# RWKV block on one core: the own part of the recurrence in one column-tiled piece, the deviation spread by small transfers, products on GpSimd, and an order given as turns

## The chip, the core and the metric

The kernel runs on one core of a Trainium2 chip. The core has five engines, each with its own instruction queue that is worked off in order: TensorE (PE in the profile; PEld is its weight load), VectorE (DVE), ScalarE (ACT), GpSimd (POOL) and SyncE (SP), which here issues nearly all DMA transfers. The metric is the device time of one launch in microseconds. Before the change three runs took 729.16, 731.47 and 731.89 us; their median is 731.47 us.

## The reference

One RWKV layer over a batch of NB = 8 sequences of T = 256 tokens with E = 512 channels, all in float32. H = 32 heads have S = 16 channels each. Every batch starts from a state of its own.

```
xn = ln(x) * ln1_w + ln1_b;   sx = shift(xn) - xn
xxx = tanh((xn + sx * maa_x) @ maa_w1)            # five groups of 32
x5 = xn + sx * (maa_stack + xxx @ maa_w2)         # five mixed inputs
w = exp(-exp(time_decay + tanh(x5[1] @ decay_w1) @ decay_w2))
r, k, v = x5[3] @ Wr.T, x5[0] @ Wk.T, x5[2] @ Wv.T
g = silu(x5[4] @ Wg.T)
for t in range(T):                                # per head, s is 16 x 16
    a = outer(k[t], v[t])
    out[t] = r[t] @ (u * a + s)                   # u = faaaa
    s = a + w[t] * s
att = (out - mean) * rsqrt(var + eps) * gn_w + gn_b   # per head, 16 channels
x = x + (att * g) @ Wo.T
xn2 = ln(x) * ln2_w + ln2_b;  sx2 = shift(xn2) - xn2
rr = sigmoid((xn2 + sx2 * ffn_maa_r) @ ffn_Wr.T)
kk = relu((xn2 + sx2 * ffn_maa_k) @ ffn_Wk.T) ** 2
return x + rr * (kk @ ffn_Wv.T)
```

In `out[t]` the term with `u * a` needs no state: it is (sum over the head's channels of r·u·k) times v. It is called the own part below.

## The kernel before

**Layout.** Channels lie on the 128 partitions and tokens along the free axis. The 512 channels are four blocks of 128 (blk), taken in two halves q of two blocks m, so a tile of 128 x 2 x 256 holds half of a batch's tensor. k and v have one column more, a leading one, so that they are also read shifted by a token. Within a block r, k and w are stored with the head as the fast index of the partition, v and att with another order in which each head's channels stand in four groups of 32 partitions.

**Stages.** For each batch there are three stages. `inputs_of_scan` loads x, normalizes it, builds the mixed inputs (PE L608, DVE L617, POOL L619) and projects them (PE L540). `scan` runs the recurrence. `rest` normalizes per head, multiplies by the gate, projects with Wo, and runs the feed-forward part with weights that are streamed from memory for each batch into tiles Ws (PE L540 and L555). In phase p the planner may mix the inputs of batch p, the scan of batch p-1 and the rest of batch p-2.

**The scan.** v goes to a DRAM tile vo (a transfer issued by ACT), and for each block four transfers on SP (L368, the helper's `dma_start`) read it back, spread over partitions, as vs, 512 KB each. ACT L699 writes the first column of vs, DVE L702 multiplies vs with kp (in PSUM) into kv, DVE L704 runs the recurrence over 1024 columns into st, POOL L707 multiplies it by r. When the four pieces of a block are done, PE L715 sums over channels ("gather") into one half of the PSUM tile pat, and DVE L721 adds that to att. For the own part, POOL L685 multiplies r by k, a block at a time, PE L687 sums over the head with a full 128 x 128 mask hm (scaled by faaaa) into the other half of pat, and DVE L689 multiplies by v into att. There are four vs buffers, five st (st8), three att and one pat; `ps`, the pool for all other products, has three buffers.

**The deviation.** In `rest`, ACT squares att (L729), PE L736 averages the squares per head in four column tiles of 32 outputs each, one for each block, so that the result has 128 rows for the four blocks; ACT and DVE turn it into the reciprocal deviation rs (L741, L743). PE L750 spreads rs back over the channels of each head with selection masks in `con`, and DVE L757 multiplies att by it. ACT L760 applies gn_w and gn_b, POOL L762 multiplies by the gate.

**The order.** Every piece of work is recorded with an engine and a cost in us, and `Plan.order` makes a static order for all five queues, which is then emitted. `AIMS` gives each piece an aim, as numbers written into the kernel. For each engine the planner looks at the next 14 ready pieces (`AHEAD`), takes the one with the least sum of earliest start and `PULL` times aim, and among the engines the one that can start first. `safe` keeps it from taking buffers in a way that could block.

Of the kernel before, what the change touches and what calls it, by code (L numbers as in the profile page):

```python
# [10 lines left out]
ALU = mybir.AluOpType  # L11

P = 128
NB, T, E = 8, 256, 512
H, S = 32, 16
# [15 lines left out]
C_HM, C_MEAN = 0, P  # L31
# [26 lines left out]
class Plan:  # L58
# [4 lines left out]

    LATENCY = {"PE": 0.25, "DVE": 0.12, "ACT": 0.2, "POOL": 0.15, "DMA": 2.6}
    SWITCH = {"ACT": 1.3, "PE": 0.1}
    AHEAD = 14
# [32 lines left out]
    def stage(self):  # L99
# [5 lines left out]
    AIMS = """  # L105
        -172 35 -38 12 -58 44 -27 96 7 17 28 24 132 62 53 37 25 19 18 194 65 220 8 -18 5 -33 -10 -4 -14 -2
        8 136 74 286 35 35 95 34 10 214 26,
        -186 -106 -126 -144 -123 -108 -71 -55 -105 -91 -92 -149 -126 -130 -97 -116 -129 -42 -103 -116 -154
        -126 -118 -6 -12 2 -49 -3 -7 -57 -40 -48 -50 -64 -58 -55 -58 -10 -3 -65 -58 -51 -28 -71 -61 91 12
        4 -363 5 -8 22 32 -10 22 32 45 22 73 30 22 24 30 49 33 9 11 3 -59 20 -1 11 7 19 -3 -13 -8 -9 -5 8  # L110
        16 -2 30 21 10 26 65 38 70 69 50 21 18 16 43 18 44 22 32 6 40 34 42 56,
        30 18 23 20 21 -6 -4 25 -44 -32 21 7 -6 34 23 28 34 35 -41 20 10 35 23 31 41 15 55 5 24 46 34 50
        53 51 53 53 55 59 30 -18 73 4 63 -33 -11 62 -37 42 16 69 90 85 97 57 95 118 106 128 115 101 67 101
        74 106 101 93 62 78 -75 71 97 75 91 14 19 102 43 52 88 57 107 86 75 101 89 104 125 129 117 110 120
        115 -30 40 111 -51 -2 75 151 133 131 142 147 153,
        32 41 24 26 25 3 12 27 13 57 51 42 -4 36 88 11 55 11 -63 66 84 81 58 66 99 105 66 103 98 18 124
        118 99 84 80 118 -39 34 131 -30 52 97 107 14 50 145 -40 20 57 140 146 146 156 117 158 168 161 169
        173 127 119 158 121 152 154 123 -7 24 53 15 51 128 153 99 102 151 121 136 145 119 130 155 138 170
        180 171 175 163 184 253 175 94 110 151 129 106 116 158 135 199 184 87 188 200,
        37 -9 36 36 159 135 183 163 107 51 134 38 95 161 143 171 187 185 94 180 185 193 172 176 185 198  # L120
        168 184 190 187 192 265 188 181 172 199 198 206 217 185 194 202 197 155 193 247 169 193 158 186
        232 229 241 199 207 253 240 232 244 150 174 231 181 253 241 210 241 243 177 225 227 246 223 252
        243 248 233 238 248 237 210 218 254 249 253 262 264 239 140 277 282 276 223 217 152 189 221 216
        253 230 238 252 270 283,
        174 178 166 199 155 188 210 268 184 279 224 264 257 279 276 292 298 289 152 278 282 297 276 285
        247 300 289 297 299 296 309 287 294 282 273 306 312 316 318 319 313 287 311 235 262 350 326 324 75
        283 322 325 326 306 319 345 351 345 341 292 307 333 268 294 335 307 282 290 248 324 311 308 311
        348 338 341 334 337 332 216 267 329 331 345 341 321 285 333 321 353 335 310 360 360 348 351 349
        326 273 294 373 283 318 382,
        281 278 270 328 330 288 340 354 258 298 309 287 275 356 277 342 376 375 295 273 368 375 362 369  # L130
        371 373 370 371 380 376 390 386 375 366 361 383 366 378 364 364 384 306 379 355 383 414 409 402
        338 418 411 410 422 381 410 433 439 431 437 378 406 414 384 397 419 412 417 409 321 430 409 408
        410 412 418 410 404 418 406 380 420 422 439 436 419 412 458 436 435 478 445 443 382 390 434 346
        374 418 441 451 459 441 450 465,
        359 355 361 343 374 358 405 409 363 373 376 361 357 418 408 442 435 454 371 425 440 442 448 447
        434 450 442 442 445 439 442 451 453 426 425 471 384 430 479 450 479 446 473 453 461 436 484 478
        479 463 489 474 500 458 498 514 494 502 518 474 518 502 476 442 464 497 379 454 387 479 467 483
        473 494 487 469 486 486 473 473 468 496 478 499 529 487 487 503 492 493 540 507 524 546 513 549
        550 518 503 545 559 514 533 550,
        416 412 423 422 424 375 477 509 425 478 512 449 432 518 411 525 528 514 464 492 547 531 531 538  # L140
        530 529 517 521 541 540 387 507 533 525 492 535 488 557 559 482 547 517 512 466 508 561 534 553
        441 549 547 560 574 538 576 559 582 577 599 569 570 544 556 586 548 557 548 548 411 572 577 509
        557 538 563 555 574 575 539 484 567 529 584 604 588 581 585 591 586 591 585 574 441 492 529 344
        463 535 607 597 627 634 591 601,
        -75 -13 35 -2 34 48 26 39 75 -14 39 41 44 78 -3 38 48 27 53 71 45 28 31 80 75 43 66 76 51 36 29 33
        60 100 78 72 86 57 72 61 80 86 76 25 8 104 73 43 -13 125 80 82 70 -34 -14 55 69 40 30 59 82 35 78
# [72 lines left out]
    def sequence(self, phases):  # L219
        self.ops = []  # L220
        rows = [row.split() for row in self.AIMS.split(",")]
        for p, phase in enumerate(phases):
# [3 lines left out]
            for kind, i in phase:  # L226
# [3 lines left out]
                for op, op.rank in zip(lot, map(int, aims)):  # L230
                    pass
# [664 lines left out]
```

## Time and profile before

| what | us | share of the span |
|---|---|---|
| median of three runs | 731.47 | |
| the profiled execution | 735.19 | |
| its span, first to last instruction | 733.1 | |
| PE busy | 673.4 | 92% |
| DVE busy | 595.4 | 81% |
| POOL busy | 558.0 | 76% |
| ACT busy | 345.6 | 47% |
| own part on PE, DVE, POOL (L687, L689, L685) | 20.3, 13.0, 20.5 | |
| spreading the deviation on PE, DVE (L750, L757) | 9.1, 10.5 | |

The granted clock of PE was 0.968 of full speed over the span. A busy time is what an engine's instructions cover; since matmuls overlap, the mean of one matmul is longer than the time that it adds. An idle time ("idle before") belongs to the engine in front of the instruction, and behind the arrow stands what ended it.

### The profile page before, as it was taken

The page shows a single profiled execution, that of the slowest core. Times are in us where ns is not written, and L with a number is a line of the kernel's source. Part 1 is how long each engine was busy: PE and PEld are TensorE (multiplying, and loading weights), DVE is VectorE, ACT ScalarE, POOL GpSimd, SP SyncE. Part 2 cuts the span into 40 slices and gives each one's busy share as a digit, 9 for nine tenths or more (in the row PEclk, how much of TensorE's full clock was granted, in tenths as well). Part 3 has the DMA queues.
Part 4 walks back from the last instruction along what each step waited for, and adds up shares of the span by engine and source line. Part 5 has one row for each costly group of instructions (what it writes and reads, how often), then busy time and mean ns, then how long its engine had stood idle before and what let it go on. Part 6 is the DMA issues. An engine that isn't in the chain of part 4 may idle for free. (4 is left out here: it accounts for less than half of the span.)

```text
span 733.1 us, 10498 instructions
## 1 busy us (share of the span) xinstructions
PE 673.4 (92%) x3744; PEld 446.6 (61%) x3744; DVE 595.4 (81%) x612; ACT 345.6 (47%) x705; POOL 558.0 (76%) x462
## 2 busy tenths in 40 slices
PE   4899699889989989999999999999988999799997
PEld 3676376647756567547764686648755666545453
DVE  1559999999999998889699978999888799798120
ACT  4256334335755156524773555626634236434441
POOL 4557976887996788878887997789876778779351
PEclk9899799989999998999999999999999799999999
DMA  8686456447666567763958539662973338873542
GB/s 294 230 233 170 116 136 148 99 110 203 168 159 187 176 160 185 180 212 99 218 169 245 173 100 259 161 190 86 252 211 98 87 99 212 221 218 113 173 143 86
DMA packets 53891, 124.23 MB, mean 169 GB/s; under 512 B 7440, under 2 KB 12432, under 8 KB 53840
## 3 DMA queue, kind: packets, MB, share of 16 engines
q1 hardware_dynamic: 49232, 119.38, 59.6%
q10 hardware_dynamic: 4608, 4.20, 1.9%
q8 instruction: 29, 0.48, 0.3%
q14 instruction: 22, 0.18, 0.1%
HBM read 115.16 MB, written 8.39 MB: 169 GB/s over the span
## 5 line engine op out<-in xcount | busy, mean ns | idle before, releaser
L707 POOL TENSOR_TENSOR st<-st,r 128x1024 f32<-128x1024 f32 x128 | 301.5, 2359 | 75.7 <-DVE st L704 71.4
L704 DVE TENSOR_TENSOR_SCAN st<-wrep,kv 128x1024 f32<-128x1024 f32 x128 | 292.0, 2281 | 8.4 <-PE pat L715 1.2
L702 DVE TENSOR_TENSOR kv<-vs,kp 128x1024 f32<-128x1024 f32 x128 | 156.7, 1224 | 19.6 <-ACT vs L699 16.6
L555 PE MATMUL ps<-Ws,mix 128*128 128x512 f32 x256 | 117.6, 600 | 5.4 <-DMA Ws<-in_fr 2.5
L619 POOL TENSOR_TENSOR mix<-mix,xn 128x512 f32<-128x512 f32 x80 | 86.4, 1092 | 28.5 <-DVE mix L617 26.4
L699 ACT ACTIVATE vs<-s,cm 128x4 f32<-128x4 f32 x128 | 38.1, 298 | 135.7 <-DMA vs<-vo 133.6
L617 DVE SCALAR_TENSOR_TENSOR mix<-ps,vec,sx 128x256 f32<-128x256 f32 x160 | 68.5, 474 | 20.2 <-PE ps L608 13.9
L555 PEld LDWEIGHTS ps<-Ws,mix 128*128 128x128 f32 x256 | 46.8, 190 | 59.2 <-issue 48.0
L715 PE MATMUL pat<-st,con 128*32 128x256 f32 x1024 | 68.8, 395 | 3.2 <-DVE att L689 2.3
L540 PE MATMUL ps<-mix,Wk 128*128 128x256 f32 x256 | 65.0, 405 | 2.8 <-DVE att L757 2.1
L540 PE MATMUL ps<-mix,Wg 128*128 128x256 f32 x256 | 61.4, 394 | 2.4 <-DVE mix L617 1.6
L540 PE MATMUL ps<-mix,Ws 128*128 128x256 f32 x256 | 59.1, 383 | 3.4 <-ACT g L663 1.7
L540 PE MATMUL ps<-mix,Wr 128*128 128x256 f32 x256 | 60.5, 383 | 1.3 <-ACT w L645 0.6
L540 PEld LDWEIGHTS ps<-mix,Wk 128*128 128x128 f32 x256 | 50.0, 201 | 15.4 <-issue 6.1
L540 PE MATMUL ps<-mix,Wv 128*128 128x256 f32 x256 | 59.0, 381 | 0.0
L555 PE MATMUL ps<-Ws,g 128*128 128x512 f32 x128 | 58.0, 599 | 0.9 <-DMA Ws<-in_wo 0.5
L540 PEld LDWEIGHTS ps<-mix,Wg 128*128 128x128 f32 x256 | 49.5, 197 | 12.8 <-issue 2.4
L540 PEld LDWEIGHTS ps<-mix,Ws 128*128 128x128 f32 x256 | 47.8, 190 | 13.8 <-POOL mix L527 3.8
L540 PEld LDWEIGHTS ps<-mix,Wr 128*128 128x128 f32 x256 | 47.6, 190 | 11.7 <-issue 3.9
L527 POOL TENSOR_TENSOR mix<-mix,xn 128x512 f32<-128x512 f32 x48 | 51.7, 1092 | 3.9 <-ACT mix L525 3.9
L715 PEld LDWEIGHTS pat<-st,con 128*32 128x32 f32 x1024 | 32.6, 112 | 36.3 <-issue 8.5
L540 PEld LDWEIGHTS ps<-mix,Wv 128*128 128x128 f32 x256 | 48.1, 190 | 9.2 <-issue 2.5
(79 smaller groups left out, 839.1 us busy)
## 6 DMA issues: line engine op xcount, KB each, us to landing
vs<-vo SPq DMA_DIRECT2D x128, 512.0 KB, 4.8
Ws<-in_wo SPq DMA_DIRECT2D x32, 256.0 KB, 4.6
Ws<-in_fv SPq DMA_DIRECT2D x32, 256.0 KB, 4.4
Ws<-in_fk SPq DMA_DIRECT2D x32, 256.0 KB, 4.4
Ws<-in_fr SPq DMA_DIRECT2D x32, 256.0 KB, 4.2
xt<-in_x SPq DMA_DIRECT2D x16, 256.0 KB, 4.4
x<-in_x SPq DMA_DIRECT2D x16, 256.0 KB, 4.8
vo<-v ACTq DMA_DIRECT2D x32, 128.0 KB, 4.6
```

Source lines behind the costliest of these rows:

```text
L527: gp(512, t, [t, xn[q]], lambda q=q, t=t: nc.gpsimd.tensor_tensor(t(), t(), xn[q]()[:, :, 1 : T + 1], ALU.add), 1.8)
L540: nc.tensor.matmul(ps()[:, m, :], lhsT=w[k]()[:, o : o + P], rhs=src[k // 2]()[:, k % 2, :], start=(k == 0), stop=(k == NK - 1),)
L555: nc.tensor.matmul(ps().rearrange("p m t -> p (m t)"), lhsT=src[h]()[:, k % 2, n * P : (n + 1) * P], rhs=w[k](), start=(k == 0), stop=(k = ...
L617: dve(256, [t], [p_, vec, sx[q]], lambda g=g, q=q, m=m, t=t, p_=p_: nc.vector.scalar_tensor_tensor(t()[:, m, :], p_()[:, m, :], col(f"maa_ ...
L619: gp(512, t, [t, xn[q]], lambda q=q, t=t: nc.gpsimd.tensor_tensor(t(), t(), xn[q]()[:, :, 1 : T + 1], ALU.add), 1.8)
L699: act(4, vs, [s0, cm], lambda i=i, blk=blk, vs=vs: nc.scalar.activation(vs()[:, :, 0:1], s0()[:, blk, 4 * i : 4 * i + 4].rearrange("p (n o ...
L702: dve(4 * T, [kv], [vs, kp], lambda m=m, vs=vs, kv=kv, kp=kp: nc.vector.tensor_tensor(kv(), vs(), kp()[:, m : m + 1, :].to_broadcast([P, 4 ...
L704: dve(4 * T, [st], [w, kv], lambda w=w, kv=kv, st=st: nc.vector.tensor_tensor_scan(st().rearrange("p n t -> p (n t)"), w().rearrange("p n ...
L707: gp(4 * T, st, [st, r], lambda m=m, st=st, r=r: nc.gpsimd.tensor_tensor(st(), st(), r()[:, m : m + 1, :].to_broadcast([P, 4, T]), ALU.mult))
L715: nc.tensor.matmul(pat()[32 * i : 32 * i + 32, 0, :], lhsT=con()[:, s : s + 32], rhs=done[i]()[:, j, :], start=(j == 0), stop=(j == 3),)
```

## The change

The own part is computed for a whole batch at once: two products r·k of double width on POOL, one piece on PE of four column tiles (masks of 32 columns, one tile for each block) into a `ps` tile, and a copy on ACT to a tile c, whose row block of 32 partitions holds what one block of channels needs. From c, eight small transfers per half q, of 32 partitions by 256 columns (32 KB), write each row block to all four groups of 32 partitions of att; POOL then multiplies att by v. L687 and L689 and the second half of pat's use go away.

The deviation is spread in the same manner in batches 0 to 6: eight transfers per half copy rs into a tile rsb (the second sq tile or an rk tile), and POOL multiplies att by it. The last batch keeps the masks on PE and the product on DVE. The constants are laid out anew for both: in each, a head's value now stands on four neighbouring rows.

The planner is a plain one: `TURNS` gives each of the 2730 pieces a turn, the ready piece with the lowest turn is taken next whatever its engine, and a piece that finds no buffer is put off until one comes free. `AHEAD`, `PULL` and `safe` are gone. All small transfers are on SP's queue. The turns themselves, 25 rows of numbers in place of the aims, are not shown; of the planner's old lines only those that stay are.

```diff
 NVEC = len(VECS)
-C_HM, C_MEAN = 0, P
+C_HM, C_MEAN = 0, 32
 C_SUM = C_MEAN + 32
 C_SEL = C_SUM + P
 NCONST = P + C_SEL + 2 * P
...
     def sequence(self, phases):
+        rows = iter(self.TURNS.split(","))
+        turns = {0: next(rows)}
+        for kind in range(3):
+            for p in range(NB):
+                turns[next(i for k, i in phases[p + kind] if k == kind and i)] = next(rows)
         self.ops = []
...
+        for i, turn in turns.items():
+            lot, turn = self.stages[i], turn.split()
+            assert len(turn) == len(lot)
+            for op, t in zip(lot, turn):
+                op.rank = int(t)
+            self.ops += lot
+        for op in self.ops:
             for b in op.bufs:
                 b.left += 1
...
     def order(self, phases):
         self.sequence(phases)
         free = dict.fromkeys(self.LATENCY, 0.0)
...
+        mode, done, queue, put_off = dict.fromkeys(free), [], [], []
+        for n, op in enumerate(self.ops):
+            op.number, op.waits = n, len(op.before)
             if not op.waits:
...
+                heapq.heappush(queue, (op.rank, n))
+        while queue:
+            op = self.ops[heapq.heappop(queue)[1]]
             at = max(free[op.engine], op.ready)
             need = {}
             for b in op.bufs:
                 if b.place is None:
...
+                    need[b.pool] = need.get(b.pool, 0) + 1
+            at = max([at] + [sorted(s[0] for s in self.pools[p])[n - 1] for p, n in need.items()])
+            if at == float("inf"):
+                put_off.append(op)
+                continue
             if op.mode and op.mode != mode[op.engine]:
                 at += self.SWITCH[op.engine]
...
+                mode[op.engine] = op.mode
             for b in op.bufs:
                 if b.place is None:
...
+                    b.slot = max((s for s in self.pools[b.pool] if s[0] <= at), key=lambda s: s[0])
+                    b.slot[0], b.place = float("inf"), b.slot[1]
             op.start, op.end = at, at + op.us
             free[op.engine] = op.end
             for b in op.bufs:
...
                 b.until = max(b.until, op.end + op.lag)
                 if b.pool and not b.left:
                     b.slot[0] = b.until
+                    for o in put_off:
+                        heapq.heappush(queue, (o.rank, o.number))
+                    put_off = []
             for o in op.after:
                 same = o.engine == op.engine and op.lag < 1
                 o.ready = max(o.ready, op.end + (0.03 if same else op.lag))
                 o.waits -= 1
                 if not o.waits:
...
+                    heapq.heappush(queue, (o.rank, o.number))
             done.append(op)
...
+        if len(done) < len(self.ops):
+            raise RuntimeError("no piece of work can start: too few buffers")
         self.span = max(op.end for op in done)
         return sorted(done, key=lambda op: op.start)
...
-    hm = const("hm", [P, NK, P])
+    hm = const("hm", [P, NK, 32])
...
-    pool("rk", 1, [P, T])
+    pool("rk", 2, [P, 2, T])
+    pool("c", 1, [P, T])
...
     def head_masks():
         for k in range(NK):
-            dve(128, [hm], [con, vec], lambda k=k: nc.vector.tensor_scalar(
-                hm()[:, k, :], con()[:, C_HM : C_HM + P], col("faaaa", k), None, ALU.mult))
+            dve(32, [hm], [con, vec], lambda k=k: nc.vector.tensor_scalar(
+                hm()[:, k, :], con()[:, C_HM : C_HM + 32], col("faaaa", k), None, ALU.mult))
...
         load(s0, state[:, b], 32)
         dve(64, [cm], [s0], lambda: nc.vector.tensor_reduce(cm(), s0(), op=ALU.add, axis=mybir.AxisListType.X))
         act(4, cm, [cm], lambda: nc.scalar.mul(cm(), cm(), -1.0 / S))
+        rks, pc, c = [], new("ps", f"pc{b}"), new("c", f"c{b}")
+        for q in range(NQ):
+            r, k, rk = got["r", q], got["k", q], new("rk", f"rk{b}_{q}")
+            gp(512, rk, [r, k], lambda rk=rk, r=r, k=k: nc.gpsimd.tensor_tensor(rk(), r(), k()[:, :, 1 : T + 1], ALU.mult), 1.85)
+            rks.append(rk)
+        def mm():
+            for blk in range(NK):
+                nc.tensor.matmul(
+                    pc()[32 * blk : 32 * blk + 32, 0, :], lhsT=hm()[:, blk, :], rhs=rks[blk // 2]()[:, blk % 2, :],
+                    start=True, stop=True)
+        pe(0.53, [pc], [hm, *rks], mm, "columns", [c])
+        act(256, c, [pc], lambda: nc.scalar.copy(c(), pc()[:, 0, :]))
         for blk in range(NK):
             q, m = divmod(blk, 2)
             if m == 0:
-                got["att", q] = new("att", f"att{b}_{q}")
+                att, v = new("att", f"att{b}_{q}"), got["v", q]
+                for n in range(2):
+                    for i in range(4):
+                        rows = slice(32 * i, 32 * i + 32)
+                        dma(att, lambda blk=2 * q + n: c()[32 * blk : 32 * blk + 32, :],
+                            lambda n=n, att=att, rows=rows: att()[rows, n, :], 32, c)
+                gp(512, att, [att, v], lambda att=att, v=v: nc.gpsimd.tensor_tensor(
+                    att(), att(), v()[:, :, 1 : T + 1], ALU.mult), 1.85)
+                got["att", q] = att
             att, r, k, v, ew = (got[what, q] for what in ("att", "r", "k", "v", "w"))
             vo = new("vo", f"vo{b}_{blk}")
             plan.add("ACT", 0.5, [vo], [v], lambda m=m, v=v, vo=vo: nc.scalar.dma_start(
...
             if m == 0:
                 kp = new("kp", f"kp{b}_{q}")
                 act(512, kp, [k], lambda k=k, kp=kp: nc.scalar.copy(kp(), k()[:, :, 0:T]))
-            w, rk, pat = (new(p_, f"{p_}{b}_{blk}") for p_ in ("wrep", "rk", "pat"))
+            w, pat = (new(p_, f"{p_}{b}_{blk}") for p_ in ("wrep", "pat"))
             act(4 * T, w, [ew], lambda m=m, w=w, ew=ew: nc.scalar.activation(
                 w()[:, :, 1:T], ew()[:, m : m + 1, 0 : T - 1].to_broadcast([P, 4, T - 1]), AF.Exp, scale=-1.0), "exp")
-
-            gp(256, rk, [r, k], lambda m=m, rk=rk, r=r, k=k: nc.gpsimd.tensor_tensor(
-                rk(), r()[:, m, :], k()[:, m, 1 : T + 1], ALU.mult), 1.85)
-            pe(0.43, [pat], [hm, rk], lambda blk=blk, pat=pat, rk=rk: nc.tensor.matmul(
-                pat()[:, 1, :], lhsT=hm()[:, blk, :], rhs=rk(), start=True, stop=True), into=[att])
-            dve(256, [att], [pat, v], lambda m=m, att=att, pat=pat, v=v: nc.vector.tensor_tensor(
-                att()[:, m, :], pat()[:, 1, :], v()[:, m, 1 : T + 1], ALU.mult))
             done = []
             for i in range(4):
...
             dve(256, [att], [pat, att], lambda m=m, att=att, pat=pat: nc.vector.tensor_tensor(
                 att()[:, m, :], pat()[:, 0, :], att()[:, m, :], ALU.add))
+    def by_block(t):
+        return t() if len(t().shape) == 3 else t().rearrange("p (m t) -> p m t", m=2)
     def rest(b, got):
         sqs = []
         for q in range(NQ):
...
         act(256, rs, [pv, eh], lambda: nc.scalar.activation(
             rs()[:, 0:T], pv()[:, 0, :], AF.Sqrt, bias=eh()[:, 0:1]), "sqrt", 1)
         dve(256, [rs], [rs], lambda: nc.vector.reciprocal(rs()[:, 0:T], rs()[:, 0:T]), 6.25)
-        pr = [new("ps", f"psr{b}_{q}") for q in range(NQ)]
-
-        def mm():
-            for m in range(2):
-                for q in range(NQ):
-                    rows, s = slice(64 * q, 64 * q + 64), C_SEL + m * P
-                    nc.tensor.matmul(
-                        pr[q]()[:, m, :], lhsT=con()[rows, s : s + P], rhs=rs()[rows, 0:T], start=True, stop=True)
-
-        pe(0.97, pr, [con, rs], mm, "rows64")
+        if b == NB - 1:
+            pr = [new("ps", f"psr{b}_{q}") for q in range(NQ)]
+            def mm():
+                for m in range(2):
+                    for q in range(NQ):
+                        rows, s = slice(64 * q, 64 * q + 64), C_SEL + m * P
+                        nc.tensor.matmul(
+                            pr[q]()[:, m, :], lhsT=con()[rows, s : s + P], rhs=rs()[rows, 0:T], start=True, stop=True)
+            pe(0.97, pr, [con, rs], mm, "rows64")
         ys = []
         for q in range(NQ):
-            att, g, ps = got["att", q], got["g", q], pr[q]
-            dve(512, [att], [ps, att], lambda att=att, ps=ps: nc.vector.tensor_tensor(att(), ps(), att(), ALU.mult))
+            att, g = got["att", q], got["g", q]
+            if b == NB - 1:
+                dve(512, [att], [pr[q], att], lambda att=att, ps=pr[q]: nc.vector.tensor_tensor(att(), ps(), att(), ALU.mult))
+            else:
+                rsb = new("rk", f"rsb{b}_{q}") if q else sqs[1]
+                for n in range(2):
+                    for i in range(4):
+                        rows = slice(32 * i, 32 * i + 32)
+                        dma(rsb, lambda blk=2 * q + n: rs()[32 * blk : 32 * blk + 32, 0:T],
+                            lambda n=n, rows=rows, rsb=rsb: by_block(rsb)[rows, n, :], 32, rs)
+                gp(512, att, [att, rsb], lambda att=att, rsb=rsb: nc.gpsimd.tensor_tensor(
+                    att(), att(), by_block(rsb), ALU.mult), 1.85)
             for m in range(2):
                 blk = 2 * q + m
                 act(256, att, [att, vec], lambda m=m, blk=blk, att=att: nc.scalar.activation(
...
-    load(con, consts[:, P:NCONST], 464)
+    load(con, consts[:, P:NCONST], 224)
...
-    con[:, C_HM : C_HM + P] = head[:, None] == head_v[None, :]
-    for h in range(HB):
-        con[:, C_MEAN + h] = (head_v == h) / S
+    con[:, C_HM : C_HM + 32] = head[:, None] == np.arange(32)[None, :] // 4
+    con[:, C_MEAN : C_MEAN + 32] = (head_v[:, None] == np.arange(32)[None, :] // 4) / S
     for i in range(4):
         for h in range(HB):
             con[:, C_SUM + 32 * i + 4 * h + i] = head == h
-            con[32 * i + h, C_SEL + P * (i % 2) : C_SEL + P * (i % 2 + 1)] = head_v == h
+            con[32 * i + 4 * h, C_SEL + P * (i % 2) : C_SEL + P * (i % 2 + 1)] = head_v == h
     same = head_v[:, None] == head_v[None, :]
```

## The prediction

> **What bounds the kernel now.** I read the busy totals first, then the stretch in which the scans run, then the groups of instructions that the change touches, then SP's queue. The page's first part gives the totals over the span of 733.1 us:
>
> ```profile
> PE 673.4 (92%) x3744; PEld 446.6 (61%) x3744; DVE 595.4 (81%) x612; ACT 345.6 (47%) x705; POOL 558.0 (76%) x462
> ```
>
> Three engines are close together, so I looked for the stretch that sets the period. The first product of the recurrence starts at 47.8 us, and the last sum into the result of the recurrence ends at 679 us. Busy time between the two (columns: length, then busy us and instructions of each engine, granted clock, DMA share, GB/s):
>
> ```profile
> 48.00:679.00 631.00, 591.93 (x3411) 395.76 (x3410) 570.32 (x558) 305.75 (x626) 515.00 (x392) 0.97 0.62 166
> ```
>
> The reader is to see that eight batches take 631 us here, 78.9 us each. PE idles for 39 us, DVE for 61 and POOL for 116. PE is the tightest and DVE next. Before this stretch lie 48 us of loading and first projections, behind it 54 us of the last batch's tail. The groups that the change removes, replaces or resembles (busy us, mean ns of one | idle before):
>
> ```profile
> L619 POOL TENSOR_TENSOR mix<-mix,xn 128x512 f32<-128x512 f32 x80 | 86.4, 1092 | 28.5 <-DVE mix L617 26.4 <-PE ps L555 1.9
> ...
> L685 POOL TENSOR_TENSOR rk<-r,k 128x256 f32<-128x256 f32 x32 | 20.5, 642 | 2.7 <-PE pat L687 1.9 <-ACT r L653 0.7
> ...
> L687 PE MATMUL pat<-rk,hm 128*128 128x256 f32 x64 | 20.3, 398 | 2.5 <-DVE att L721 2.3
> L762 POOL TENSOR_TENSOR g<-g,att 128x512 f32<-128x512 f32 x16 | 20.2, 1275 | 9.9 <-ACT att L760 9.9
> ...
> L689 DVE TENSOR_TENSOR att<-pat,v 128x256 f32<-128x256 f32 x32 | 13.0, 408 | 3.8 <-PE pat L687 3.6
> ...
> L757 DVE TENSOR_TENSOR att<-ps,att 128x512 f32<-128x512 f32 x16 | 10.5, 677 | 2.8 <-PE ps L750 2.8
> ...
> L750 PE MATMUL ps<-sq,con 64*128 64x256 f32 x64 | 9.1, 402 | 2.8 <-DVE mix L617 1.1 <-DVE o L793 1.0 <-ACT mix L777 0.7
> ...
> L736 PE MATMUL ps<-sq,con 128*32 128x256 f32 x64 | 5.1, 391 | 0.0
> ```
>
> Here the busy total matters, not the mean: matmuls overlap. L687 computes 32 products in 20.3 us, 0.63 us each. L736 computes as many in 5.1 us, because its four 32-column pieces run together. Last, SP's waits and its issues (issue times as min/median/max ns):
>
> ```profile
> SPq L368 <- DVE kv L702: 209.3, 74, 8.4
> SPq L368 <- DMA vo<-v: 84.8, 11, 21.7
> SPq L368 <- DMA vs<-vo: 49.6, 22, 4.8
> ```
>
> ```profile
> L368 SPq DMA_DIRECT2D vs<-vo x128: 514/520/1667, 42.7 to 653.0; - x128
> ...
> L368 SPq DMA_DIRECT2D s<-in_state x8: 328/334/2132, 2.1 to 503.1; - x8
> ```
>
> ```profile
> vs<-vo SPq DMA_DIRECT2D x128, 512.0 KB, 4.8
> ...
> s<-in_state SPq DMA_DIRECT2D x8, 32.0 KB, 2.5
> ```
>
> SP mostly waits for a vs buffer to come free. The 32 KB load of the state is the only row of the size that the change adds: 0.33 us to issue, 2.5 us to land.
>
> **The change, part by part.**
>
> *Own part on PE and DVE.* Out go 32 full-width products (L687, 20.3 us of PE) and 32 products with v on DVE (L689, 13.0). In come eight groups of four column tiles, of the shape of L736: 8 x 0.64 = 5.1. So PE -15.2 and DVE -13.0, both wholly within the stretch. Eight copies of c on ACT at 0.38 us (the 128x256 ACT row from PSUM at L588, mean 381 ns) are 3.0 us, hidden in ACT's 325 idle us; without that cover each lengthens the way from rk to the result by 0.4. PE also loses its waits in pat: 2.3 us for L689 and 2.3 for L721. Bounds -4.6 to 0; I take 0, since waits tend to return in another place.
>
> *Own part on POOL.* 32 products r·k at 0.642 (20.5) become 16 at double width. The nearest row is L619, with one operand of rows of T+1: 1.092 us, 17.5 in all. The 16 products att·v are new, same row: 17.5. POOL +14.5.
>
> *Deviation, batches 0 to 6.* Out go seven eighths of L750 (9.1 x 7/8 = 8.0 us of PE) and 14 products L757 at 0.677 (9.5 us of DVE). In come 14 POOL products with both operands unbroken rows, as in L762: 14 x 1.275 = 17.9. Here a rule speaks against the change. The Trainium skill ("GPSIMD Engine Reference", section 4.1, Engine selection) wants elementwise products on VectorE and gives GpSimd about twice the time for two inputs. The rows agree on the price (1275 against 677 ns). By the rule, which counts the engine's own time, both moves cost +32.4 us (14.5 + 17.9) if POOL sets the end, 765. By the stretch, POOL goes to 515 + 32.4 = 547 us, under PE's 592 - 23.2 = 569. I take the stretch.
>
> *Small transfers.* 8 x 16 for c and 7 x 16 for rs make 240, all on SP: 240 x 0.33 = 80 us of issue on top of about 150 (128 x 0.52 and 209 at 0.4), in a queue that has some 500 us of waiting. They move 7.9 MB beside 124. What stands behind them on SP are vs, the streamed weights, x and out. A vs is issued when its buffer is freed, and DVE takes one each 631/128 = 4.9 us, so the three other buffers give 14.8 us of cover; issue, landing and the column from ACT take 0.52 + 4.8 + 0.3 = 5.6. So SP may be held for 9 us unseen. A group of eight in a lump takes 8 x 0.33 = 2.7; without the cover, 240 x 0.33 = 80 us would be on the path. The second rule: the Trainium skill ("DMA: Bandwidth & Descriptors", Rules for kernel authors) says that transfers under 64 KB are mostly overhead and should be joined. [...] If all eight of a group stood on the path one by one, that is 8 x (0.33 + 2.5) = 22.6 us; issued one behind the other without waiting, 2.7 + 2.5 = 5.2. No row shows two transfers into one tile. I take 5.2 as the group's own need, since SP's row shows issues every 0.4 us to other tiles; the other end is a rival below.
>
> *What the longer ways delay.* In the rest, rs reaches att through L750 and L757 in 1.1 + 1.3 = 2.4 us now, and then in 5.2 + 2.6 = 7.8: +5.4 per batch, while the next batch's scan and the one after's projections fill the engines. Without that cover it would be 7 x 5.4 = 38; the last batch, which has none, keeps the old way. For c the order matters: by the turns, the list of POOL has 0 to 4 pieces, in most cases one L707 (2.36 us), between the last transfer of a group and the product that waits for it. Issue and landing take 2.8, so some 0.5 us of stall at each of about 23 such places (16 for att, 7 for rs): 11 us. If landing takes a vs's 4.8 us instead, it is 2.8 each, 64. Behind the waiting product are queued L707, which frees st8 buffers for the scan and feeds the gather, and the sums L619, for which PE's projections wait. POOL already waits 71.4 us for the scan, and a stall that falls there costs nothing. Bounds 0 to 64; I take half of 11, 6 us, since the state's row is the nearer in size.
>
> *Order and masks.* A new hand order replaces the aims everywhere. No row prices it. It can't gain more than PE's 39 idle us; if every period idled PE as the stretch's first 82 us do (11.0), it would lose 8 x 11 - 39 = 49. I take 0. Masks of 32 columns take under 1 us from DVE in the start, and the smaller constants nothing; both lie beside loads.
>
> *Sum.* In the stretch PE loses 15.2 + 8.0 = 23.2 (569), DVE 13.0 + 9.5 = 22.5 (548), POOL gains 32.4 (547). Both of the tight engines shrink alike, so with PE's 39 idle us kept the stretch is 608. With 6 us of POOL stalls it is 614, and the span 733.1 - 23.2 + 6 = 716. The profiled execution ran 735.2 us, 2.1 around the span, and would become 718; the median of the runs is 3.7 lower, so I forecast **714 us**.
>
> **Rivals.**
> 1. *POOL eats the gain.* At 547 of 608 us it is 90% busy (82% now), in order and with late products: stalls at 23 places of 0.8 us, off the scan's waits, are 18 us, leaving 731.5 - 23 + 18 = 726 or a little over. For it: the 26.4 us that POOL now waits for L617. Against: POOL's idle is still 61 us.
> 2. *SP becomes the bound, slower.* If each small transfer waits for the one before it into the same tile, SP is held 2.5 + 0.33 a step. A batch has 24 such steps (16 for att, 8 in which the two rs groups alternate), 68 us, and 42 older issues of 0.41, 17: 85 us against 78.9. Eight times 85 plus 48 and 54 is 782. It decides from (79 - 17)/24 = 2.6 us per step. For it: SP waits 49.6 us for landings of vs already. Against: other issues stand between most steps, and cover part of the landing.
> 3. *Products late, slower.* Landing behind the 512 KB transfers takes 4.8 us or more. Then the sum into att holds the one pat, the gather behind it holds four of the five st8, and the scan stands: 16 places of 2.4 us, 38 us, make 731.5 - 23 + 38 = 746.
> 4. *The order gains too*, by a quarter of PE's 39 us, with no stalls: 731.5 - 23 - 10 = 698.
>
> **How the numbers follow.** A run of this kernel varies by about 0.5% (729.2 to 731.9), 3.7 us, which I take for "same". The forecast has 0.50 (704 to 722 by itself), rival 4 0.10, rival 1 0.22, of which a third ends between 728 and 735, rival 2 0.08, rival 3 0.10. So faster 0.50 + 0.10 + 0.14 = 0.74, same 0.08, slower 0.18. The range reaches into rival 4 at the low end and up to rival 3 at the high end, 702 to 746. About 0.06 lies below it and 0.12 above.
>
> **What would show it.** L687's successor at 5 us, L689 gone and L757 with two instructions; POOL near 590 busy, PE near 650, DVE near 572; the stretch from first kv to last sum near 614. Small transfers landing in about 2.5 us. Wrong, if POOL's products wait more than 20 us for landings, if DVE's wait for vs (16.6 us for ACT's column now) passes 30, or if SP waits for the small transfers themselves.

## The result, and the profile after

The changed kernel takes 707.84 us (median of four runs; 701.38 to 713.32) against 731.68 before, 23.8 us less. The run of 713.32 us fell in a slower state (granted clock 0.966 against 0.974 to 0.983 in the others), so the ratio, 0.965 with an interval of 0.957 to 0.973, is that of the other three, whose median is 705.88 us. In a second comparison, on the chip that the first four experiments share, it took 702.79 against 729.69, ratio 0.964 (0.956 to 0.972). The forecast was 714, in a range of 702 to 746.

The profiled execution ran 705.88 us with a span of 704.1. First the busy totals of the page after the change:

```profile
PE 652.3 (93%) x3688; PEld 431.5 (61%) x3688; DVE 578.6 (82%) x566; ACT 349.4 (50%) x719; POOL 587.7 (83%) x476
```

PE lost 21.1 us, DVE 16.8, and POOL gained 29.7. The stretch from the first kv to the last sum into att is now 46.3 to 650.5 us; the second line is the tail (columns as before: length, busy us of PE, PEld, DVE, ACT, POOL, granted clock, DMA share, GB/s):

```profile
46.30:650.50 604.20, 571.62 (x3377) 380.83 (x3375) 553.49 (x515) 308.46 (x638) 547.53 (x410) 0.99 0.75 191
650.50:704.10 53.60, 45.33 (x132) 22.56 (x132) 8.93 (x13) 17.40 (x32) 17.15 (x20) 0.98 0.40 131
```

The stretch fell from 631 to 604.2, by 26.8 us, which is nearly all of the span's 29.0; the start lost 1.7 and the tail 0.5. Within the stretch PE works 20.3 us less and idles 32.6 us instead of 39. POOL works 32.5 more and idles 57 instead of 116. The groups that take the place of those shown before the change:

```profile
L701 POOL TENSOR_TENSOR att<-att,v 128x512 f32<-128x512 f32 x16 | 17.5, 1094 | 2.5 <-DMA att<-c 1.6 <-DMA s<-in_state 0.8
...
L681 POOL TENSOR_TENSOR rk<-r,k 128x512 f32<-128x512 f32 x16 | 17.4, 1094 | 0.0
...
L794 POOL TENSOR_TENSOR att<-att,sq 128x512 f32<-128x512 f32 x7 | 9.0, 1288 | 1.1 <-DMA sq<-sq 1.1
L794 POOL TENSOR_TENSOR att<-att,rk 128x512 f32<-128x512 f32 x7 | 9.0, 1282 | 0.0
...
L686 PE MATMUL ps<-rk,hm 128*32 128x256 f32 x64 | 5.9, 389 | 0.2 <-issue 0.2
...
L786 DVE TENSOR_TENSOR att<-ps,att 128x512 f32<-128x512 f32 x2 | 1.3, 686 | 1.8 <-PE ps L778 1.8
L778 PE MATMUL ps<-sq,con 64*128 64x256 f32 x8 | 1.1, 402 | 0.0
```

The durations are those of the rows that the forecast took them from: 1094 ns against L619's 1092, 1285 against L762's 1275, and 5.9 us for PE's own part against 5.1. What stands behind the second bar is the important part. POOL's 30 new products wait 1.6 + 0.8 + 1.1 = 3.5 us for transfers, all told; the 0.8 is put down to the state's load, which this product doesn't read, so it may belong to a transfer of c. Then SP: its waits, its issues (min/median/max ns) and the landings (KB, median us):

```profile
SPq L373 <- DVE kv L725: 83.7, 44, 5.3
SPq L373 <- DMA vo<-v: 59.2, 14, 9.5
...
SPq L373 <- DMA vs<-vo: 13.1, 12, 3.7
```

```profile
L373 SPq DMA_DIRECT2D vs<-vo x128: 513/557/1642, 41.0 to 622.8; - x128
L373 SPq DMA_DIRECT2D att<-c x128: 507/585/1119, 61.2 to 631.8; - x128
L373 SPq DMA_DIRECT2D rk<-sq x56: 507/588/1132, 127.4 to 611.8; - x56
L373 SPq DMA_DIRECT2D sq<-sq x56: 507/588/1581, 128.0 to 608.7; - x56
```

```profile
att<-c SPq DMA_DIRECT2D x128, 32.0 KB, 4.0
...
rk<-sq SPq DMA_DIRECT2D x56, 32.0 KB, 3.6
sq<-sq SPq DMA_DIRECT2D x56, 32.0 KB, 3.5
```

A small transfer costs SP 0.59 us, as much as a 512 KB one, and not the 0.33 of the state's load; 240 of them are some 141 us of issue. SP waits 84 us for free vs buffers instead of 209, and nothing in its list of waits is the landing of a small transfer. That slack was consumed, but DVE saw none of it: its wait for ACT's column of vs fell from 16.6 to 8.2 us.

### The profile page after: what moved, and what is told of

It is laid out like the page before. It is cut to its first block, busy times and chain, and to the rows that moved or that the text cites. A ratio compares the mean times of both kernels' runs of the same rounds, so it can differ in the third digit from the quotient of the medians.

```text
span 704.1 us, 10753 instructions
## 1 busy us (share of the span) xinstructions
PE 652.3 (93%) x3688; PEld 431.5 (61%) x3688; DVE 578.6 (82%) x566; ACT 349.4 (50%) x719; POOL 587.7 (83%) x476
## 4 chain that ended last, share of the span: by engine, by line
PE 42%; DVE 12%; POOL 9%; DMA 8%; ACT 4%; issue 4%; SPq 0%; POOLq 0%; DVEq 0%; ACTq 0%
PE ps L546 17%; PE ps L561 15%; DVE st L727 6%; DMA vs<-vo 5%; PE pat L738 4%; DVE kv L725 4%; POOL st L730 4%; PE ps L614 2%; DMA vo<-v 1%; DVE mix L623 1%; PE ps L511 1%; PE ps L576 1%; POOL mix L533 1%; POOL g L800 1%; POOL rs L496 1%
## 5 line engine op out<-in xcount | busy, mean ns | idle before, releaser
L730 POOL TENSOR_TENSOR st<-st,r 128x1024 f32<-128x1024 f32 x128 | 300.7, 2358 | 24.7 <-DVE st L727 23.2
L561 PE MATMUL ps<-Ws,mix 128*128 128x512 f32 x256 | 119.1, 608 | 5.7 <-issue 1.1
L625 POOL TENSOR_TENSOR mix<-mix,xn 128x512 f32<-128x512 f32 x80 | 86.5, 1093 | 13.2 <-DVE mix L623 12.6
L722 ACT ACTIVATE vs<-s,cm 128x4 f32<-128x4 f32 x128 | 36.6, 296 | 111.1 <-DMA vs<-vo 102.4
L623 DVE SCALAR_TENSOR_TENSOR mix<-ps,vec,sx 128x256 f32<-128x256 f32 x160 | 69.1, 472 | 16.8 <-PE ps L614 16.6
L546 PE MATMUL ps<-mix,Ws 128*128 128x256 f32 x256 | 61.3, 397 | 11.3 <-DMA Ws<-in_fk 4.1
L738 PE MATMUL pat<-st,con 128*32 128x256 f32 x1024 | 64.3, 382 | 1.2 <-POOL st L730 0.6
L546 PEld LDWEIGHTS ps<-mix,Ws 128*128 128x128 f32 x256 | 50.0, 199 | 22.2 <-POOL mix L533 5.3
L546 PE MATMUL ps<-mix,Wg 128*128 128x256 f32 x256 | 59.8, 384 | 3.1 <-ACT xn L517 1.1
L546 PE MATMUL ps<-mix,Wv 128*128 128x256 f32 x256 | 62.0, 393 | 0.1
L546 PE MATMUL ps<-mix,Wk 128*128 128x256 f32 x256 | 60.6, 391 | 0.8 <-ACT g L669 0.8
L546 PEld LDWEIGHTS ps<-mix,Wg 128*128 128x128 f32 x256 | 47.4, 190 | 14.6 <-issue 3.9
```

Source lines behind the costliest of these rows:

```text
L546: nc.tensor.matmul(ps()[:, m, :], lhsT=w[k]()[:, o : o + P], rhs=src[k // 2]()[:, k % 2, :], start=(k == 0), stop=(k == NK - 1),)
L561: nc.tensor.matmul(ps().rearrange("p m t -> p (m t)"), lhsT=src[h]()[:, k % 2, n * P : (n + 1) * P], rhs=w[k](), start=(k == 0), stop=(k = ...
L623: dve(256, [t], [p_, vec, sx[q]], lambda g=g, q=q, m=m, t=t, p_=p_: nc.vector.scalar_tensor_tensor(t()[:, m, :], p_()[:, m, :], col(f"maa_ ...
L625: gp(512, t, [t, xn[q]], lambda q=q, t=t: nc.gpsimd.tensor_tensor(t(), t(), xn[q]()[:, :, 1 : T + 1], ALU.add), 1.8)
L722: act(4, vs, [s0, cm], lambda i=i, blk=blk, vs=vs: nc.scalar.activation(vs()[:, :, 0:1], s0()[:, blk, 4 * i : 4 * i + 4].rearrange("p (n o ...
L730: gp(4 * T, st, [st, r], lambda m=m, st=st, r=r: nc.gpsimd.tensor_tensor(st(), st(), r()[:, m : m + 1, :].to_broadcast([P, 4, T]), ALU.mult))
```

## The experiments

Theory A is that of the forecast: the gain is engine time taken from PE and DVE in the stretch, and the order and the longer ways matter little. Theory B gives the gain to the order. Others are named where they are tested.

**The changed kernel again (e1).** No edit.

> The changed kernel unaltered, as the level for the others of this call. Both theories: 0.957 to 0.973 of before, 700 to 713 us.

702.79 us, ratio 0.964 (0.956 to 0.972). This is the level for the next three, which ran on the same chip.

**The deviation as before (e3).** All batches take the masks on PE and the product on DVE. The turns of the transfers and products go; PE's piece gets the turn of the first transfer, DVE's the next two.

```diff
-        if b == NB - 1:
+        if True:
             pr = [new("ps", f"psr{b}_{q}") for q in range(NQ)]
...
-            if b == NB - 1:
+            if True:
                 dve(512, [att], [pr[q], att], lambda att=att, ps=pr[q]: nc.vector.tensor_tensor(att(), ps(), att(), ALU.mult))
```

> The deviation by masks on PE and by DVE in all eight batches, the own part as changed, the order by turns. Theory A: PE +8 and DVE +9.5 come back, POOL loses 18, the time rises by 6 to 10 over the unaltered one, 713 to 718. Theory B: less than 3. Theory C, POOL is the real bound after the change: the time falls, since POOL is freed of 18 us.

721.99 us, 0.988 of before (0.981 to 0.994), so 19.2 more than e1. First the stretch of e1 and that of this kernel (columns as above), then one of DVE's waits and one of PE's (us in total, times, longest us), then the two restored groups:

```profile
46.60:646.50 599.90, 568.11 (x3374) 378.08 (x3372) 553.57 (x515) 308.48 (x638) 546.64 (x409) 0.99 0.74 192
45.60:663.00 617.40, 577.63 (x3428) 383.78 (x3427) 561.55 (x529) 307.34 (x638) 530.00 (x395) 0.99 0.69 180
```

```profile
DVE att L792 <- PE ps L784: 17.8, 8, 6.4
...
PE ps L620 <- DVE att L792: 4.3, 3, 1.4
```

```profile
L792 DVE TENSOR_TENSOR att<-ps,att 128x512 f32<-128x512 f32 x16 | 10.3, 685 | 17.8 <-PE ps L784 17.8
...
L784 PE MATMUL ps<-sq,con 64*128 64x256 f32 x64 | 9.1, 402 | 1.5 <-ACT g L675 0.7 <-ACT k L665 0.7
```

In the stretch PE works 577.6 us (568.1 in e1), so the 8 us of L750's kind do come back; POOL works 17 less (530 against 547), and the time rises all the same. Theory C, POOL as the bound, falls. But the rise is twice what theory A allowed. In the two profiled stretches, 17.5 us apart, PE's work accounts for 9.5 us and its idle time for 8.0 (39.8 against 31.8). DVE stands 17.8 us in front of PE's product, and PE in turn stands 5.9 us until DVE's product is done (4.3 of them in the line shown), which it did nowhere in e1's stretch. So the restored pieces bring back waits beside their work. That they stand too close together in the order is my reading; no other turns were tried for them.

**The own part as before, and both parts as before (e2, e4).** The old code of the own part, with masks of 128 columns and a buffer `rko` for r·k, in the order of the turns. The restored pieces get turns inside their block: r·k at the first kv, PE's product and DVE's product one after the other at the third scan.

```diff
-    pool("rk", 2, [P, 2, T])
-    pool("c", 1, [P, T])
+    pool("rk", 1, [P, 2, T])
+    pool("rko", 1, [P, T])
...
-    hm = const("hm", [P, NK, 32])
+    hm = const("hm", [P, NK, P])
...
+            gp(256, rk, [r, k], lambda m=m, rk=rk, r=r, k=k: nc.gpsimd.tensor_tensor(
+                rk(), r()[:, m, :], k()[:, m, 1 : T + 1], ALU.mult), 1.85)
+            pe(0.43, [pat], [hm, rk], lambda blk=blk, pat=pat, rk=rk: nc.tensor.matmul(
+                pat()[:, 1, :], lhsT=hm()[:, blk, :], rhs=rk(), start=True, stop=True), into=[att])
+            dve(256, [att], [pat, v], lambda m=m, att=att, pat=pat, v=v: nc.vector.tensor_tensor(
+                att()[:, m, :], pat()[:, 1, :], v()[:, m, 1 : T + 1], ALU.mult))
```

> The own part as before (32 full-width products on PE, 32 products on DVE, r*k by the block), the deviation spread by transfers, the order by turns; the restored pieces get turns between the pieces that they belong to. Theory A, the gain is engine time in the stretch: PE +15 and DVE +13 come back, the time rises by 13 to 17 over the unaltered one, to 718 to 725. Theory B, most of the gain is the new order: it rises by less than 6, to below 714.

> The work of the kernel before (own part and deviation both as before) in the order of the turns. Theory A: within 5 us of before, 725 to 735, since the order gives little. Theory B: the order alone brings most of the gain, 705 to 716.

757.75 us (1.037, 1.031 to 1.044) and 769.91 us (1.054, 1.048 to 1.061). Both theories missed. The old work in the order by turns is 40 us slower than the kernel before, and neither the engine time nor the order gives that. DVE's largest wait for the restored pieces in e2 (3.6 us in the kernel before) says what is wrong with the first placement:

```profile
DVE att L702 <- PE pat L700: 54.5, 26, 5.0
```

**The same with the restored pieces apart (e5, e6).** These and the last two experiments share another chip, on which the kernel before takes 730.32 us. Only turns change: r·k some 3.5 us earlier, PE's product at the second scan, DVE's product 2.5 us of turns behind it (turns are hundredths of a us in this reckoning). The start of the first batch's scan:

```diff
-        504 3212 3775 3651 4173 3313 4419 5327 5328 3911 4376 4419 4543 4779 4116 4692 4779 4902 5138 4526 5091
+        504 3212 3775 3651 4173 3313 4069 4902 5152 3911 4376 4419 4543 4779 4116 4692 4779 4902 5138 4526 5091
```

> As the kernel with the old own part, but its restored pieces stand apart in the order: r*k some 3.5 us earlier on POOL, PE's product early in the block, DVE's product 2.5 us of turns behind it. Theory A (engine time, and the 54.5 us that DVE waited for PE's product in the first version came of back-to-back turns): DVE's waits for that product fall below 25 us and the time to 718 to 732. Theory D (in this order the full-width products cannot be served without stalls, wherever they stand): above 740.

> The work of the kernel before in the order of the turns, the restored pieces spaced as in the kernel with the old own part spaced. Theory A: 727 to 745, near the kernel before. Theory B (the order alone brings the gain): below 716. Theory D: above 750.

744.33 us (1.020, 1.015 to 1.026) and 761.56 us (1.044, 1.038 to 1.050). DVE's wait for that product fell from 54.5 to 4.6 us, and some 13 us came back in e5. The rest did not: e5 lies above the 740, and e6 above the 750, from which theory D (the full-width products can't be served in this order) was to hold. In e5's stretch PE works 591.7 us, 23.6 more than in e1's, of which the own part's own products make 14.4, and idles 49.7, 17.9 more. PE's waits in e5 (us in total, times, longest us) show where the idle time went:

```profile
PE pat L728 <- DVE att L702: 17.9, 15, 2.6
...
PE pat L700 <- DVE att L734: 6.4, 7, 2.8
```

There is one pat. The old own part keeps one half of it until DVE has multiplied, so the gather stands (17.9 us), and the next product stands until DVE has summed (6.4). In the kernel before, whose list was made for this, the two were 2.3 us each. With two placements tried, and none tuned, theory D isn't proven; what is shown is that these pieces don't fit this list without more work.

**The new work in the old order (e7).** The work of the changed kernel and the plain planner, but the turns are the starts that the old planner had given; the new pieces stand where those stood that they replace, the transfers some 6 us ahead of the old product for c, and from the old PE piece on for rs.

```diff
     TURNS = """
-        388 546 520 716 1391 2629 2130 1030 2539 2040 1301 1769 2858 2767 1497 1211 2358 5506 1859 4936 2914 2933
+        90 2098 313 881 223 2438 430 2937 790 1014 1736 1556 3335 2757 2576 2348 1646 1465 1104 3697 3225 3593
...
```

> The work of the changed kernel in the order of the kernel before: the plain planner with the starts that the old planner gave as turns, the new pieces put where the pieces stood that they replace, transfers some 6 us ahead. Theory A: the engine time is saved in this order too, 705 to 722. Theory E (the gain needs the new order, because the longer ways of c and rs stall a list that was made for short ones): 728 or more.

829.84 us, 1.138 of before (1.129 to 1.146): the slowest of all. Theory A falls here, and the time is where theory E put it. That the plain planner, given these starts, makes the old kernel's time with the old work was not run. The stretch of this kernel, then waits of it (us in total, times, longest):

```profile
48.30:776.40 728.10, 606.96 (x3359) 391.14 (x3358) 555.47 (x513) 306.42 (x634) 547.66 (x408) 0.91 0.59 156
```

```profile
ACT att L810 <- POOL att L806: 53.9, 9, 12.9
DVE kv L737 <- ACT vs L734: 48.8, 18, 12.9
...
PEld ps L573 <- POOL g L812: 37.8, 6, 9.4
...
POOL att L806 <- DMA sq<-sq: 35.6, 5, 9.1
PE ps L573 <- POOL g L812: 33.1, 4, 8.6
```

DVE and POOL work as long as in the changed kernel (555 and 548 us), but PE idles 121 us, and its work takes 607.0 us instead of 571.6, at a granted clock of 0.91. One batch shows how; a piece of the order in time, start and length in us (SP's transfers alone, and those that wait for them, directly or behind another):

```profile
415.81 1.74 DVE L782 RECIPROCAL sq<-sq 128x256 f32<-128x256 f32 x1
417.61 0.55 SPq L385 DMA_DIRECT2D sq<-sq  x1
...
430.15 0.56 SPq L385 DMA_DIRECT2D vs<-vo  x1
430.75 0.60 SPq L385 DMA_DIRECT2D sq<-sq  x1
...
435.16 1.26 POOL L806 TENSOR_TENSOR att<-att,sq 128x512 f32<-128x512 f32 x1 [7.98 <-DMA sq<-sq]
...
436.45 1.09 ACT L810 ACTIVATE att<-att,vec 128x256 f32<-128x256 f32 x2 [12.87 <-POOL att L806]
437.69 1.26 POOL L812 TENSOR_TENSOR g<-g,att 128x512 f32<-128x512 f32 x1 [1.27 <-ACT att L810]
...
441.20 0.47 ACT L734 ACTIVATE vs<-s,cm 128x4 f32<-128x4 f32 x2
...
441.70 1.23 DVE L737 TENSOR_TENSOR kv<-vs,kp 128x1024 f32<-128x1024 f32 x1 [5.77 <-ACT vs L734]
...
443.68 2.05 PE L573 MATMUL ps<-Ws,g 128*128 128x512 f32 x2 [8.31 <-POOL g L812]
```

The reciprocal ends at 417.55, and the product on POOL starts at 435.16, 17.6 us later: SP issues the sixteen transfers with vs and weights between them. POOL, ACT and PE each stand in their queues in front of the piece that needs it. Behind ACT's piece stand the first columns of vs (L734), so DVE's recurrence stands as well, 5.8 us. In the changed kernel the same way is longer: between the end of the reciprocal and the product lie 22.8 to 29.7 us in the seven batches. There PE's waits hold only this for the gated product:

```profile
PE ps L561 <- POOL g L800: 5.2, 3, 3.3
```

So the order by turns does not shorten the way. It puts other work on every queue while the way lasts, and PE waits 5.2 us in all for its end. The old order, made for a spread of 3.9 us (in its last batch, from the reciprocal's end at 683.82 to the product's at 687.73), has the consumers too early.

**The last batch too by transfers (e8).**

```diff
-        if b == NB - 1:
+        if b == NB:
...
-            if b == NB - 1:
+            if b == NB:
```

> The last batch too spreads its deviation by 16 transfers and two products on POOL. Working of the prediction: no cover there, the tail from the last sum into att to the end grows by 5.4 us (53.6 in the changed kernel). Theory with issue as measured (0.59 us each, landing 3.5): 16 issues, 9.4, and 3.5 and 2.6, against 2.4: up to 13 us. Rival: the tail is filled by other work, less than 2 us.

722.81 us in one run; its comparison is the tail in the trace, 67.3 us (653.7 to 721.0) against 53.6, so 13.7 more, with a granted clock of 0.88 in it against 0.98. The forecast's 5.4 and the rival's 2 are both too little; the reckoning with the measured issue time, up to 13, comes near. While the sixteen go out nothing else is on SP, and its timeline (start us, us, instruction) shows the bare price of the transfers:

```profile
656.27 1.75 DVE L784 RECIPROCAL sq<-sq 128x256 f32<-128x256 f32 x1 [2.53 <-ACT sq L782]
658.08 0.51 SPq L387 DMA_DIRECT2D sq<-sq  x1
658.65 0.58 SPq L387 DMA_DIRECT2D rk<-sq  x1
...
667.50 0.59 SPq L387 DMA_DIRECT2D rk<-sq  x1
668.88 1.26 POOL L808 TENSOR_TENSOR att<-att,sq 128x512 f32<-128x512 f32 x1 [13.84 <-DMA sq<-sq]
670.10 1.26 POOL L808 TENSOR_TENSOR att<-att,rk 128x512 f32<-128x512 f32 x1
```

Sixteen issues go out 0.63 us apart, 10.0 us in all, none waiting for another to land, though eight go into the same tile. From the reciprocal's end (658.02) to the end of the second product (671.36) pass 13.3 us, against 3.1 in the changed kernel's last batch (654.76 to 657.90). That is 10.2 of the 13.7; most of the rest is PE's clock behind the wait, shown in the last section.

**Not tried.** More work on one engine at a time, in the order unchanged (PE's piece five times, one kv in eight twice, r·k twice), and each small transfer issued twice, would show how near POOL, DVE and SP are to being the bound. None was run, so that stays open. No run gave a version faster than the changed kernel.

## Why the prediction was right, and where its sizes were off

Direction and mechanism held: the stretch set the time before and sets it now, PE's work in it fell, and the fall is in the span. By its steps:

- *Engine time.* PE: own part 20.3 to 5.9 (forecast 5.1), deviation 9.1 to 1.1; in the stretch 20.3 of the 23.2 us. POOL: +32.5 in the stretch, forecast +32.4. DVE fell by 16.8 and not by 22.5, although its 46 instructions are gone. In its timeline many an instruction starts some 0.1 us before the one ahead of it ends. Over the span the durations sum to 627.9 us before and 606.7 after, the busy total is 595.4 and 578.6, so 4.4 us of overlap went with the instructions; and the masks took 3.4 us where they took 1.4. A sum of durations overstates what leaves a busy total.
- *The rule for elementwise work.* By the Trainium skill's rule that elementwise products belong on VectorE ("GPSIMD Engine Reference", section 4.1, Engine selection), the forecast's estimate for the moves was +32.4 us, 765. The trace agrees on the price, about twice (1285 against 686 ns), but the profiled execution took 705.9: the longer product on an engine with 116 idle us was cheaper than the shorter one on an engine with 61.
- *POOL's stalls, +6.* This step failed in size: 3.5 us of waits for transfers. One of them, 1.1 us in the seventh batch, lies in a way that does reach PE, which stands 3.3 us there for the gated product. The forecast put about 0.5 us on each of 23 places, since the turns leave one POOL piece between the last transfer and its product. Landings took 3.5 to 4.0 us, longer than the assumed 2.5, and were still over when POOL came; that POOL runs later against SP than the turns say is my reading, not a test.
- *Small transfers.* 0.59 us of issue and not 0.33, some 141 us and not 80. The row that stood for them is a load from DRAM; the new ones copy from SBUF to SBUF, in another shape, and which of the two makes the difference no run tells. It lengthened the way, but no wait of DVE or PE shows that SP's time ran out. The Trainium skill's rule that transfers under 64 KB are mostly overhead ("DMA: Bandwidth & Descriptors", Rules for kernel authors) agrees with the trace, where one of 32 KB takes SP as long as one of 512 KB. It decides only where SP or the way is on the path, as in e8.
- *The longer way.* +5.4 per batch is about half of what came: the bare way is 13.3 us against 3.1 (e8), +10.2. The forecast's 5.2 counts eight issues of 0.33 and a landing; the two groups of a batch alternate on SP, so that the first product waits for fifteen issues, 0.63 us apart. In the covered batches the way takes 23 to 30 us. "Without that cover it would be 38" was the weakest number in the forecast: e7, with much of the cover gone, lies 100 us above the kernel before, though not by the length of the way alone.
- *Order, 0, and the waits in pat, 0.* PE's idle time in the stretch fell by 6.5 us, where the forecast kept all 39. Before the change PE stood three times behind the product on DVE that is gone; the two longest of these waits (us in total, times, longest us):

```profile
PE ps L540 <- DVE att L757: 2.1, 1, 2.1
...
PE ps L608 <- DVE att L757: 1.6, 1, 1.6
```

  The three make 4.2 us. With the waits at L750 (2.8) and the two in pat (2.3 each), 11.6 us of PE's idle time stood at the removed pieces or behind them. Afterwards L686 waits 0.2, and 5.2 for the gated product are new. That would make the fall, but other waits moved as well, and what the order gave no run separates. To price it as a term of its own was the wrong frame. The old work in the new order is 31 us slower than before (e6), the new work in the old order 100 us slower (e7), both together 24 us faster. In these static in-order lists, work and order are one edit; what the order alone is worth stays open, since neither mixed kernel had its own tuned list.
- *The sum.* 718 was forecast for the profiled execution, and 705.9 came. Of the 12 us between, 9.6 lie in the stretch (614 against 604.2): 6 of stalls that did not come and 6.5 of idle time, less the 2.9 of PE's work that stayed. 2.2 lie in the start and the tail. The median is off by less, 6 us, because the profiled execution was 3.7 above it before and 2.0 below it after.
- *Rivals.* POOL as the eater of the gain: not seen, e3 freed it and lost. SP bound by transfers that wait for each other: refuted by the 0.63 us rhythm in e8. Late products holding pat and the scan: next to nothing in the changed kernel (the sum into att waits 0.9 us for POOL), but it is what e7 shows in part (15.1 us there). The order gains too, 698: without the 6 us of stalls and with 6.5 us less idle time on PE, where this rival had 10 and the forecast 0, the result lies between the two; whether it was the order is open, as said.

## What to carry to other kernels

Take work off the engine that is tight in the stretch that sets the end, even where the move doubles its price and lengthens its way by 20 us, but only together with an order that puts other work on every queue behind it. What a long way costs depends on where its consumers stand in their queues: here ways of 23 to 30 us cost PE 5.2 us of waiting for the gated product, and in e7, where the way shown is shorter, 33.1 us. Look at the wait of the consumers, and at what stands behind them. An old piece put back into a list made without it tells of the pair, not of the piece.

## What the runs showed of the hardware that I had not expected

- A 32 KB transfer from SBUF to SBUF takes SP 0.59 us to issue in the median, where a 32 KB load from DRAM took 0.33 before and 0.43 in the changed kernel. The landing differs little between the two kinds and more between the kernels: in the changed kernel, with a DMA share of 0.75 in the stretch, att from c takes 4.0 us and the load from DRAM 4.1; in e7, at 0.59, they take 2.6 and 2.8; before, at 0.62, the load took 2.5. That it is the load on the DMA engines that sets it is my reading.
- PE's granted clock goes with its idle time: 0.99 in the stretch of the changed kernel with 5% idle, 0.97 before with 6%, 0.96 in e6 with 8%, 0.91 in e7 with 17%, 0.88 in e8's tail with 30%. The tail of e8 shows which comes first. PE stands 13 us in front of the gated product; then come that stand without the moments at its ends, the time behind it, and the time after that (columns as above, clock third from the end):

```profile
663.00:675.10 12.10, 0.00 (x0) 0.00 (x0) 0.00 (x0) 3.68 (x6) 4.95 (x4) 0.68 0.50 157
675.16:681.10 5.94, 5.93 (x7) 2.52 (x8) 0.00 (x0) 0.22 (x1) 0.00 (x0) 0.51 0.00 0
681.20:685.00 3.80, 3.80 (x10) 1.68 (x9) 1.42 (x3) 0.00 (x0) 0.00 (x0) 1.00 0.00 0
```

  Behind the wait seven matmuls of L575 take 5.9 us at half the clock; after them the same step takes 0.43 us and not 0.86. So PE's stall is paid a second time, some 3 us here. In e7 it is the same: behind the 8.3 us wait shown above the clock is 0.50 from 443.7 to 448.0, and over the whole run the matmuls of Ws times g cover 70.0 us instead of 59.0.
- The four masks of 32 columns took DVE 0.85 us each, where four of 128 columns had taken 0.36; e6, with 128 columns, took 0.88 each, and e7, with 32, 0.31, so it is not the width. In the changed kernel and e6 all four run beside POOL's products L625 and L623. In e7, and before, only one does (0.57 and 0.62 us); the other three take 0.50 and 0.65 us together. That POOL's product is the cause was not tested.
